# Two attention layers and two expert layers on one core: queries and keys held per sequence in a ring of four, values in nine columns a head, and expert outputs added to two sums in one tensor

## The chip, the cores and the metric

The kernel runs on one core of one Trainium2 chip. The metric is device time in microseconds (us). A core has TensorE (PE, with its weight loads shown as PEld), VectorE (DVE), ScalarE (ACT), GpSimd (POOL) and SyncE (SP), and 16 DMA engines. "SPq", "ACTq" and "POOLq" are DMAs issued from those engines.

## What is computed

Sixteen sequences of 256 tokens with 128 features pass through four layers with residuals, each on a layer norm of its input:

```python
x = x + attn_a(layernorm(x))   # 16 heads of 8, causal softmax(q k / sqrt(8)) v, projection
x = x + ffn(layernorm(x))      # 8 experts, the best two of each token, silu(x Wg) * (x Wu) @ Wd
x = x + attn_b(layernorm(x))   # 16 heads of 8, no mask
x = x + ffn(layernorm(x))      # the same expert weights
```

In attn_b the scores are an L2 form with one divisor per head and sequence:

```python
sim = -(q_row_2 - 2.0 * qk + k_col_2) / (fro_q * inf_xt)   # q_row_2 and k_col_2: maxima of a head
attn = softmax(sim)
```

The experts' outputs are weighted by the softmax of the two chosen router logits and scaled by 1/sqrt(12).

## The kernel before, in words

**Stages.** The kernel runs attention a, experts a, attention b, experts b and a last addition, one after another. Attention works on 8 blocks of 512 tokens (NT = 4 tiles of 128), that is two sequences a block. `project` (L535) loads a block (`loaded`, L522), normalizes it (`moments` L289, `normed` L303), transposes it, makes k and q with heads spread over partitions, splits each into a high and a low half in a short float format, and lays the halves by DMA (`lay`, L615) into the buffers `ks` and `qs`. There are three buffers of each, one a block, [128, 8, 512]. Eight DMAs of 256 KB lay a block: hi twice and lo twice, for k and for q. `vs` holds values with 32 columns a head, a one in the first, eight values and zeros after them.

**Rounds.** The stage is a list of 128 rounds, 16 a block and 8 a sequence; a round is one pair of heads of one sequence. In round `at` the program issues, in this order: `rows_scores` (L708), PE's scores of round `at` for the row maxima; `exponentials` (L771) of round `at - 14`, the transposed scores and ACT's exponential; `rows_maxima` (L725), one DVE reduction a round; in every second round `values` (L795) of round `at - 17`; and then the planner's steps. Row maxima are laid into spare rows of `qs` by `lay_maxima` (L740), so that the exponential's matmul subtracts them. Everything on PE, DVE, ACT, POOL and SP keeps its program order, so an instruction that waits holds up all behind it on its engine.

**The planner.** Side work is a set of generators: project, collect (L807), finish (L833), route (L332) and some set-up. Each yields how many rounds on it wants its next step, and of which kind. `due` (L866) runs at the end of each round. It takes the steps that are due, earliest first, and lets through one of kind BANK (which needs the spare PSUM banks), or two if more than two wait, and two that are not FREE (four if more than three wait). The rest come again in the next round. In attention b, project's steps stand 3, 1, 1, 2, 1, 1, 1, 1, 1, 1, 2 and 1 rounds after one another, from the load to the lay of q. Project of block n is due from round 16(n-1)-9 on in attention b, and 16(n-1)-8 in attention a (L916).

`collect` transposes the weighted values and divides by the row sums, `finish` applies the output projection and stores the block, and `route` normalizes it again, picks the two experts, and scatters each token's two rows into an HBM table by expert (POOL, eight indirect DMAs a block). In route the moments (DVE, then two small POOL operations for 1/sqrt) are followed one round later by the norm (DVE), at L337.

**Experts.** 39 tiles of 256 rows: load rows and weights, three matrix products, and POOL's indirect DMA with addition to the sums (`finish`, L1012). There are two sum tensors a layer, used in turn by the two halves of a tile; one starts as the residual, the other as zeros. `places` (L1001) makes the row numbers, with rows that no token owns sent to 128 spare rows.

**Set-up.** `prepared` (L274) sets k, q and v buffers to zero (POOL), lays ones, and is a planner task for the buffers 1 and 2, in rounds 0 to 12. `zeros` (L188) writes zeros to the sums. The last addition (from L1069) loads both sums block by block with 512-byte runs, adds and stores, all DMAs on SP's queue.

Of the kernel before, what the change touches and what calls it, by code (L numbers as in the profile page):

```python
# [42 lines left out]
P = 128  # L43
# [13 lines left out]
SEQ = 256  # L57
EPS = 1e-5
# [4 lines left out]
TOKENS = 4096  # L63
W = P + 2
# [6 lines left out]
def layers(  # L71
# [23 lines left out]
    ot = out.flatten_outer_dims().rearrange("(n t p) d -> n p t d", t=NT, p=P)  # L95
# [18 lines left out]
    def attention_weights(wq, bq, wk, bk, wv, bv, wo, bo, scale, name):  # L114
# [27 lines left out]
    blocks = ctx.enter_context(tc.tile_pool(name="blocks", bufs=4))  # L142
# [17 lines left out]
    half = const.tile([P, NE], F32, name="half")  # L160
# [14 lines left out]
    tokens = const.tile([P, NB * NT], F32, name="tokens")  # L175
    within = tokens[:, 0:ET]
    nobody = const.tile([P, 1], F32, name="nobody")
# [4 lines left out]
    totals = [  # L182
        [dram.tile([TOKENS + P, P], F32, name=f"total{i}{j}") for j in range(2)] for i in range(2)
    ]
    blank = const.tile([P, 3 * W], F32, name="blank")
    wr_sb = const.tile([P, NE], F32, name="wr_sb")

    def zeros():  # L188

        yield sy.dma_start(  # L190
            out=rows_in[NE * CAP : NE * CAP + TE, :].rearrange("(s p) d -> p s d", p=P),
            in_=blank[:, 0 : ET * W].rearrange("p (s d) -> p s d", s=ET),
        )
        for first, second in totals:
            flat = second.rearrange("(p a m) d -> p a (m d)", p=P, m=3)
            for k, m in ((0, 4), (4, 8), (8, 11)):
                to = flat[:, k:m, :]
                yield sy.dma_start(
                    out=to,
                    in_=blank[:, 0 : 3 * P].unsqueeze(1).to_broadcast([P, to.shape[1], 3 * P]),  # L200
                )
            yield sy.dma_start(out=first[TOKENS : TOKENS + P, :], in_=blank[:, 0:P])
# [3 lines left out]
    vs = [const.tile([P, NT, NH, HS], F32, name=f"v{i}") for i in range(3)]  # L206
    qs = [const.tile([P, NP, TB], F32R, name=f"q{i}") for i in range(3)]
    ks = [const.tile([P, NP, TB], F32R, name=f"k{i}") for i in range(3)]
# [30 lines left out]
    def later_constants():  # L239
# [19 lines left out]
        for t, pattern, base, by_partition in (  # L259
# [4 lines left out]
            (tokens, [[P, NB * NT]], 0, 1),  # L264
            (nobody, [[0, 1]], TOKENS, 1),
# [8 lines left out]
    def prepared(i):  # L274

        for t in (ks, qs) if i else ():
            for g in range(0, NP, 4):
                po.memset(t[i].bitcast(F32)[:, g : g + 4, :], 0.0)
                yield 1, FREE
        for j in range(2):  # L280
# [3 lines left out]
                in_=ones[0:2, :].unsqueeze(1).to_broadcast([2, NP * NT, P]),  # L284
            )
        po.memset(vs[i], 0.0)
        po.memset(vs[i].rearrange("p t h r -> p (t h) r")[:, :, 0:1], 1.0)
# [44 lines left out]
    def route(pool, psum, n, xb, free, sent):  # L332
# [4 lines left out]
        yield 1, BUSY  # L337
# [6 lines left out]
            tokens[:, n * NT : (n + 1) * NT].unsqueeze(1).to_broadcast([P, 2, NT]),  # L344
# [135 lines left out]
    def tokens_of(total, n):  # L480
        return total[n * TB : (n + 1) * TB, :].rearrange("(t p) d -> p t d", p=P)
# [27 lines left out]
    def attention(w, causal, name):  # L509
        with ExitStack() as own:  # L510
# [11 lines left out]
            def loaded(n):  # L522
# [5 lines left out]
                sy.dma_start(out=xb, in_=xt[n] if causal else tokens_of(totals[0][0], n))  # L528
                xs[n] = xb
                if not causal:  # L530
                    more = pool.tile([P, NT, P], F32, tag="more", bufs=1)
                    sy.dma_start(out=more, in_=tokens_of(totals[0][1], n))
                    return more

            def project(n):  # L535
# [38 lines left out]
                lay(ks[n % 3], halves(k, "k"), (0, 2, 1, 3))  # L574
                if causal:
                    yield 2, BANK
                    q = biased("wq", "bq", "q")
                    lay(qs[n % 3], halves(q, "q"), (0, 1, 2, 3), se if n == 0 else sy)
                else:
# [14 lines left out]
                    lay(qs[n % 3], (hi, lo), (0, 1, 2, 3), se if n == 0 else sy)  # L594
                    later(1, BUSY, constants(n, *rest))
                yield (2, BANK) if n else None
# [18 lines left out]
            def lay(to, parts, order, queue=sy):  # L615

                for i, slot in enumerate(order):
# [496 lines left out]
```

## Time and profile before

| | |
|---|---|
| median of 3 runs | 1337.88 us (1335.83 to 1341.29) |
| the profiled execution | 1343.86 us, span 1342.2 us |
| mean granted TensorE clock | 0.872 |
| busy in the span: PE, DVE, POOL, ACT | 79%, 59%, 44%, 39% |
| first scores of attention a, of attention b | 28.89, 690.46 us |
| first expert matmul, a and b | 423.69, 1088.44 us |
| issue of the last addition's first load | 1315.57 us |
| the row maxima's reduction, L222 (256 times) | 277.1 us busy |
| POOL's additions to the sums, L1019 (156 times) | 242.8 us busy |

Times in the profile are from the span's start. The attention code runs through one helper that keeps program order, so all of its instructions carry line L222 and are told apart by their tiles (mx, s, p, av, q, k). A row of the timeline gives the start, the busy time, the engine, the line, the operation, out<-in, the shape and a count; in brackets stands how long the engine was idle before, and what ended the wait. A row of busy time by stretch gives, for each engine, busy us and the number of instructions, then the granted clock, the DMA engines' share and GB/s. A busy PE is not PE at its peak.

### The profile page before, as it was taken

Reading aid. Unit: us, or ns where it says so; the run is one execution under the profiler, and the core shown is the slowest. Engines: PE = TensorE matmul, PEld = TensorE weight load, DVE = VectorE, ACT = ScalarE, POOL = GpSimd, SP = SyncE. Lnnn points to the kernel's source line nnn. Section 1 sums busy time; section 2 is a strip of 40 time slices with the busy share of each in tenths; the row PEclk is TensorE's granted clock in tenths of the full one; section 3 lists DMA queues with packets and bytes.
Section 4 is the critical chain, followed back from the end, with each engine's and each line's share of the span. In section 5 each row is a group of like instructions: output and inputs, shape, how many; then the busy total and the mean of one; then the engine's idle time right before and its main releaser. Section 6 shows DMA issues by size and latency. Waiting matters only on the chain. (4 is left out here: it accounts for less than half of the span.)

```text
span 1342.2 us, 23350 instructions
## 1 busy us (share of the span) xinstructions
PE 1066.8 (79%) x8116; PEld 771.8 (58%) x8116; DVE 787.6 (59%) x2221; ACT 518.8 (39%) x942; POOL 594.0 (44%) x599
## 2 busy tenths in 40 slices
PE   2799888898763999999457888778877459999990
PEld 1455555555543888888324454445554248888880
DVE  3667667776533555454258787888675535554541
ACT  1156445554521222222135756665555212222220
POOL 7444546655552555555330114233323325555551
PEclk9889878888855999999757999998788779999995
DMA  4244324530015877776253324133300087777757
GB/s 98 51 97 109 72 73 117 138 84 24 25 36 169 210 188 189 180 195 133 45 109 81 66 58 104 51 78 83 89 23 30 27 230 192 178 187 189 189 103 195
DMA packets 175301, 150.84 MB, mean 112 GB/s; under 512 B 14286, under 2 KB 136784, under 8 KB 175184
## 3 DMA queue, kind: packets, MB, share of 16 engines
q1 hardware_dynamic: 145310, 127.18, 34.8%
q0 software_dynamic: 26560, 18.76, 9.4%
q10 hardware_dynamic: 3314, 3.41, 1.1%
q8 instruction: 65, 1.06, 0.3%
q14 instruction: 52, 0.43, 0.1%
HBM read 82.74 MB, written 31.75 MB: 85 GB/s over the span
## 5 line engine op out<-in xcount | busy, mean ns | idle before, releaser
L1019 POOL DMA_INDIRECT total<-y,to x156 | 242.8, 1556 | 229.2 <-DVE here L1005 59.3
L222 DVE TENSOR_REDUCE mx<-s 128x6 f32<-128x768 f32 (+1 forms) x256 | 277.1, 1084 | 110.4 <-PE s L222 109.4
L222 ACT ACTIVATE p<-s 128x768 f32<-128x768 f32 (+1 forms) x256 | 232.9, 916 | 192.2 <-PE s L222 170.2
L1061 ACT ACTIVATE sg<-pg 128x256 f32<-128x256 f32 x312 | 119.4, 383 | 316.8 <-PE pg L1049 300.7
L1063 DVE TENSOR_TENSOR h<-pu,sg 128x256 f32<-128x256 f32 x312 | 131.9, 423 | 149.6 <-PE pu L1053 147.2
L222 POOL DMA_INDIRECT rows_in<-both_rows,slots x128 | 128.9, 1007 | 172.2 <-DVE both_rows L222 113.0
L1053 PE MATMUL pu<-xT,w_u 128*128 128x256 f32 x624 | 190.2, 387 | 5.7 <-DVE h L1063 5.5
L1049 PE MATMUL pg<-xT,w_g 128*128 128x256 f32 x624 | 192.6, 391 | 1.2 <-DMA w_g<-in_L_ffn_Wg_dram 0.7
L1028 PEld LDWEIGHTS py<-w_d,h 128*128 128x128 f32 x1248 | 163.8, 192 | 8.1
L1028 PE MATMUL py<-w_d,h 128*128 128x128 f32 x1248 | 164.6, 275 | 0.0
L222 PE MATMUL s<-k,q 62*128 62x256 f32 (+1 forms) x1024 | 144.3, 367 | 16.1 <-DMA k<-lo 11.4
L222 PE MATMUL s<-q,k 64*128 64x256 f32 (+1 forms) x1024 | 114.2, 307 | 42.1 <-DVE mx L222 33.5
L222 PE MATMUL av<-p,v 128*32 128x256 f32 (+1 forms) x2048 | 144.5, 406 | 0.3 <-ACT au L222 0.2
L222 PEld LDWEIGHTS s<-k,q 62*128 62x128 f32 x1024 | 89.2, 216 | 87.7 <-issue 51.8
L1053 PEld LDWEIGHTS pu<-xT,w_u 128*128 128x128 f32 x624 | 118.0, 192 | 29.6 <-DVE h L1063 13.8
L222 POOL TENSOR_SCALAR_AFFINE_SELECT p<-p 128x512 f32<-128x512 f32 x128 | 82.5, 645 | 108.3 <-ACT p L222 103.7
L222 PEld LDWEIGHTS s<-q,k 64*128 64x128 f32 x1024 | 89.5, 213 | 58.9 <-DVE mx L222 39.7
L1049 PEld LDWEIGHTS pg<-xT,w_g 128*128 128x128 f32 x624 | 102.2, 194 | 20.3 <-issue 13.8
L222 PEld LDWEIGHTS av<-p,v 128*32 128x32 f32 x2048 | 58.7, 120 | 55.2 <-issue 26.4
L222 POOL TENSOR_TENSOR lo<-to,hi 128x512 fp32r<-128x512 f32 x24 | 30.6, 1273 | 72.4 <-ACT hi L222 72.3
L996 PE MATMUL ps<-ident,x_in 128*128 128x128 f32 x156 | 30.6, 279 | 39.1 <-DMA x_in<-rows_in 39.1
L222 PE MATMUL s<-mask_q,ident_h 128*128 128x256 bf16 x256 | 58.6, 317 | 0.0
(206 smaller groups left out, 1179.3 us busy)
## 6 DMA issues: line engine op xcount, KB each, us to landing
w_g<-in_L_ffn_Wg_dram SPq DMA_DIRECT2D x78, 256.0 KB
w_u<-in_L_ffn_Wu_dram SPq DMA_DIRECT2D x78, 256.0 KB
w_d<-in_L_ffn_Wd_dram SPq DMA_DIRECT2D x78, 256.0 KB
x_in<-rows_in SPq DMA_DIRECT2D x78, 130.0 KB
k<-hi SPq DMA_DIRECT2D x32, 256.0 KB
k<-lo SPq DMA_DIRECT2D x32, 256.0 KB
q<-hi SPq DMA_DIRECT2D x28, 256.0 KB
q<-lo SPq DMA_DIRECT2D x28, 256.0 KB
```

The lines of the kernel that those rows point to most:

```text
L222: return tc.keep_in_program_order(method(*args, **kwargs))
L996: nc.tensor.transpose(ps[:, bass.ts(s, P)], x_in[:, s, 0:P], ident)
L1019: nc.gpsimd.indirect_dma_start(out=sums[(i * ET + s) % 2], out_offset=bass.IndirectOffsetOnAxis(ap=to[:, s : s + 1], axis=0), in_=y[:, s, ...
L1028: nc.tensor.matmul(py[:, s, :], lhsT=hs[c][:, bass.ts(s, P)], rhs=w_d[:, c, :], start=c == 0, stop=c == NC - 1,)
L1049: nc.tensor.matmul(pg, lhsT=w_g[:, bass.ts(c, P)], rhs=this, start=True, stop=True)
L1053: nc.tensor.matmul(pu, lhsT=w_u[:, bass.ts(c, P)], rhs=this, start=True, stop=True)
L1061: nc.scalar.activation(sg, pg, AF.Silu)
L1063: nc.vector.tensor_tensor(h, pu, sg, ALU.mult)
```

## The change

1. `ks` and `qs` become rings of four buffers, one a sequence ([128, 8, 256]). A block is laid in two parts: the first sequence where it was laid before, the second as a planner task of its own, eight rounds later (`lay_second`). Project starts at 16(n-1)-5 in attention b and 16(n-1)-3 in attention a, since a slot must be free; block 1 of attention a stays at -8. Buffers 0 and 1 are set to zero at the start, 2 and 3 in the first rounds.
2. `vs` has nine columns a head in place of 32, and one PSUM tile `av` serves a whole stage, set to zero once.
3. Route's norm comes three rounds after its moments, in place of one.
4. Each layer has one tensor with two sums, one below the other. A token's first choice adds to the first and its second choice to the second, so that each row takes one addition, and the additions are declared free of order among themselves. Rows without a token go to 8 x 128 spare rows. The first loads of the next reader wait for all additions by hand.
5. The last addition reads and stores four adjacent rows a partition (2 KB runs) and uses SP's and ACT's queues. There is a fifth block buffer and a fourth for its partner.

```diff
+RING = 4
+IDLE = 8
-    blocks = ctx.enter_context(tc.tile_pool(name="blocks", bufs=4))
+    blocks = ctx.enter_context(tc.tile_pool(name="blocks", bufs=5))
-    totals = [
-        [dram.tile([TOKENS + P, P], F32, name=f"total{i}{j}") for j in range(2)] for i in range(2)
-    ]
+    totals = [dram.tile([2 * TOKENS + IDLE * P, P], F32, name=f"total{i}") for i in range(2)]
-    vs = [const.tile([P, NT, NH, HS], F32, name=f"v{i}") for i in range(3)]
-    qs = [const.tile([P, NP, TB], F32R, name=f"q{i}") for i in range(3)]
-    ks = [const.tile([P, NP, TB], F32R, name=f"k{i}") for i in range(3)]
+    vs = [const.tile([P, NT, NH, 1 + HD], F32, name=f"v{i}") for i in range(3)]
+    qs = [const.tile([P, NP, SEQ], F32R, name=f"q{i}") for i in range(RING)]
+    ks = [const.tile([P, NP, SEQ], F32R, name=f"k{i}") for i in range(RING)]
...
     def prepared(i):
-        for t in (ks, qs) if i else ():
-            for g in range(0, NP, 4):
-                po.memset(t[i].bitcast(F32)[:, g : g + 4, :], 0.0)
+        for t in (ks[i], qs[i]):
+            if i > 1:
+                po.memset(t.bitcast(F32), 0.0)
                 yield 1, FREE
...
-        po.memset(vs[i], 0.0)
-        po.memset(vs[i].rearrange("p t h r -> p (t h) r")[:, :, 0:1], 1.0)
...
         mv, rstd = yield from moments(pool, xb)
-        yield 1, BUSY
+        yield 3, BUSY
...
+    def wait_for(load, scatters):
+        for scatter in scatters:
+            tc.add_manual_dep(
...
                 if not causal:
-                    more = pool.tile([P, NT, P], F32, tag="more", bufs=1)
-                    sy.dma_start(out=more, in_=tokens_of(totals[0][1], n))
+                    more = pool.tile([P, NT, P], F32, tag="more" if n else "o", bufs=1)
+                    second = (sy if n else se).dma_start(out=more, in_=tokens_of(totals[0], 1, n))
+                    for on in (load, second) if n == 0 else ():
+                        wait_for(on, landed)
...
-                lay(ks[n % 3], halves(k, "k"), (0, 2, 1, 3))
+                k_parts = halves(k, "k")
+                lay(n, 0, ks, k_parts, (0, 2, 1, 3))
...
-                    lay(qs[n % 3], (hi, lo), (0, 1, 2, 3), se if n == 0 else sy)
+                    q_parts = hi, lo
+                    lay(n, 0, qs, q_parts, (0, 1, 2, 3), se if n == 0 else sy)
                     later(1, BUSY, constants(n, *rest))
+                then = lay_second(n, k_parts, q_parts)
+                if n == 0:
+                    for _ in then:
+                        pass
+                else:
+                    later(8 if n > 1 else 1, FREE, then)
...
+            def lay(n, b, to, parts, order, queue=sy):
+                assert at >= (2 * n + b - RING + 1) * each // 2 + lag or 2 * n + b < RING
+                to = to[(2 * n + b) % RING].bitcast(F32)
                 for i, slot in enumerate(order):
                     queue.dma_start(
+                        out=to[slot : slot + P - SLOTS + 1 : SLOTS, :, :],
+                        in_=parts[i // 2].bitcast(F32)[:, b * SEQ : (b + 1) * SEQ],
                     )
+            def lay_second(n, k_parts, q_parts):
+                lay(n, 1, ks, k_parts, (0, 2, 1, 3))
+                yield 1, FREE
+                lay(n, 1, qs, q_parts, (0, 1, 2, 3))
...
-                            av[i * HS : (i + 1) * HS, f % 2, lo:SEQ],
+                            av[i * HS : i * HS + 1 + HD, f % 2, lo:SEQ],
...
-                for n in range(1, 3):
-                    later(8 * n - 8, FREE, prepared(n), 0)
+                for i in range(2, RING):
+                    later(0, FREE, prepared(i), 0)
...
-                later(max(0, (n - 1) * each - (8 if causal else 9)), FREE, project(n))
+                later(max(0, (n - 1) * each - (8 if n == 1 else 3 if causal else 5)), FREE, project(n))
...
-                nc.vector.tensor_scalar(here, within, left[:, i : i + 1], None, ALU.is_lt)
+                none = nobody[:, i * ET % IDLE : i * ET % IDLE + ET]
                 nc.vector.scalar_tensor_tensor(
-                    here, x_in[:, :, P], nobody, here, ALU.subtract, ALU.mult
+                    here, within, left[:, i : i + 1], none, ALU.is_ge, ALU.mult
                 )
-                nc.vector.tensor_scalar(to, here, nobody, None, ALU.add)
+                nc.vector.tensor_tensor(to, here, x_in[:, :, P], ALU.add)
...
-                    nc.gpsimd.indirect_dma_start(
-                        out=sums[(i * ET + s) % 2],
+                    add = nc.gpsimd.indirect_dma_start(
+                        out=total,
...
+                    tc.declare_no_dep(add.ins, group=group, reason="a row takes one addition")
...
+                def rows_of(of, n):
+                    return of.rearrange("(p n m) d -> n p m d", p=P, m=NT)[n]
                 for n in range(NB):
                     a = blocks.tile([P, NT, P], F32, tag="xb")
-                    nc.sync.dma_start(out=a, in_=tokens_of(sums[0], n))
-                    b = pool.tile([P, NT, P], F32, tag="b", bufs=3)
-                    nc.sync.dma_start(out=b, in_=tokens_of(sums[1], n))
+                    b = pool.tile([P, NT, P], F32, tag="b", bufs=4)
+                    for i, t, queue in ((0, a, nc.sync), (1, b, nc.scalar)):
+                        load = queue.dma_start(out=t, in_=rows_of(total[i * TOKENS : (i + 1) * TOKENS, :], n))
+                        if n == 0:
+                            wait_for(load, added)
                     nc.vector.tensor_tensor(a, a, b, ALU.add)
-                    nc.sync.dma_start(out=ot[n], in_=a)
+                    (nc.sync, nc.scalar)[n % 2].dma_start(out=rows_of(out.flatten_outer_dims(), n), in_=a)
```

## The prediction, made before the result was known

> **What bounds the kernel now.** I read the page first: slices of PE, PEclk and DMA. The span has four parts: attention a (0 to about 400 us), experts a (423 to 647), attention b (690 to 1045 with its lead-in from 652), experts b (1086 to 1310), then a tail. Busy time by stretch came second.
>
> ```profile
> core 0: us, PE busy (x) PEld busy (x) DVE busy (x) ACT busy (x) POOL busy (x), PEclk, DMA share, GB/s
> 690.00:1045.00 355.00, 283.30 (x2537) 172.38 (x2536) 271.86 (x714) 210.41 (x336) 98.16 (x109) 0.87 0.28 67
> 1317.60:1342.20 24.60, 0.00 (x0) 0.00 (x0) 5.54 (x8) 0.00 (x0) 0.00 (x0) 0.50 0.87 247
> ```
>
> Attention b has no full engine: PE 80%, DVE 77%, ACT 59%. Its engines wait for one another, in order, so a late operand delays the whole chain. The tail has no compute; its 24.6 us are DMA at 0.87 of the 16 engines. In the experts' stretch 1100 to 1200 the same view has PE at 98.68 of 100 us: TensorE sets the pace, 5.5 us a tile, and POOL's additions lie beside it.
>
> Third, the timeline of one round of attention b (PE, DVE and SP), where block 3's q is laid:
>
> ```profile
> 782.05 0.50 PE L222 MATMUL s<-k,q 62*128 62x256 f32 x4
> 784.37 0.50 PE L222 MATMUL s<-k,q 62*128 62x256 f32 x4
> ...
> 781.97 1.22 DVE L222 TENSOR_REDUCE mx<-s 128x4 f32<-128x1024 f32 x1
> 783.59 0.87 DVE L222 SCALAR_TENSOR_TENSOR lo<-to,by,hi 128x256 fp32r<-128x256 f32 x2
> 784.38 1.22 DVE L222 TENSOR_REDUCE mx<-s 128x4 f32<-128x1024 f32 x1
> ...
> 783.78 1.18 SPq L222 DMA_DIRECT2D q<-hi  x2
> 785.05 1.24 SPq L222 DMA_DIRECT2D q<-lo  x2
> ```
>
> PE makes the scores of the next round while DVE reduces this one. The reduction at 781.97 is the 42nd of the stage (round 41): block 3 starts in round 48, so its q is laid 7 rounds ahead. Fourth, attention a, where PE did wait for a lay, and where it waited behind a memset:
>
> ```profile
> 40.62 3.55 POOL L222 MEMSET k<- 128x2048 f32 x2
> 40.83 5.73 DVE L222 TENSOR_SCALAR xn<-xb,mv,rstd 128x128 f32<-128x128 f32 x4
> 46.13 1.09 PE L222 MATMUL ps<-ident,xn 128*128 128x128 f32 x4 [5.33 <-DVE xn L222]
> ...
> 63.80 1.24 SPq L222 DMA_DIRECT2D q<-hi  x2
> 65.14 1.18 SPq L222 DMA_DIRECT2D q<-lo  x2
> 71.16 0.72 PE L222 MATMUL s<-k,q 62*128 62x128 f32 x4 [1.88 <-DMA q<-lo]
> ```
>
> So a lay of 1 MB releases PE 7.4 us after its first issue and 4.8 us after its last (66.32 to 71.16), and a wait for it is real.
>
> **Part 1: the ring of four.** A block has 16 rounds. I walked the planner's list by its rules, round by round, before and after. Before, the walk gives q's lay 7 rounds ahead for blocks 2 to 7 of attention b, as the trace has it. After, project starts 21 rounds ahead of its block, not 25. Its steps need 16 rounds if nothing holds them, so q could be laid 5 ahead. But they now fall on the rounds in which collect, finish and route want the one BANK step a round (and route itself ends two rounds later), and the delay grows from 2 rounds to 5. Offsets of the lay from the block's first round:
>
> - block 2: q -3; second sequence k +5, q +6
> - block 3: q -1; k +7, q +8
> - blocks 4 to 7: q 0; k +8, q +9
>
> The second sequence's scores start in round +8. A step runs after its round's scores. So in rounds 0 (blocks 4 to 7), 8 and 9 the scores read the slot's old contents. That moves only the maxima, which shift the softmax, and costs nothing. The next round reads the new data, and PE waits for the DMA with exponentials and values queued behind it. That wait is the main new cost:
>
> - First q. From the reduction's start (781.97) lo is done 2.49 us on and the four issues are over 4.32 us on (786.29). Landing after the last issue is unseen for half the bytes: at most 4.8 (the whole 1 MB above), at least 2.5 (the page's median for a small row scatter); I take 3.0, towards the smaller since the bytes halve. Scores 0.5: next reduction at 7.8 instead of 2.4 (784.38). Loss 5.4 us in blocks 3 to 7; block 2 has three rounds and loses none.
> - Second k, blocks 4 to 7: issued when the round's scores are done (T), four issues of 0.6, landing 3, scores 0.5: T+5.9. Normal: T+1.8+2.8 (a round) = T+4.6. Loss 1.3.
> - Second q stands on SP's queue behind the next block's k (its hi after ACT, its lo after POOL): projection to T+2.1, an exponential 1.0, to 0.69 and hi 0.62 give about T+4.6, POOL's lo 1.27 behind a row scatter 1.3 gives T+7.2, q's four issues T+9.6, landing and scores T+13.1. Normal after the k's loss is T+8.7: loss 4.4 in blocks 4 to 6. Block 3's k is in time, so its normal is T+4.6 and it loses 8.5. Block 7 has no next k: it loses 3.1.
>
> Sum: 13.9 + 3 x 11.1 + 9.8 = 57 us. Low end 25: SP starts sooner than I think, or idle time of DVE (23%) gives half back. High end 90: landing 4.8, and half clock after each wait (the same score group takes 0.79 us at the stage's slow moments, 0.50 at its fast ones). In attention a the walk puts q 5 to 8 ahead and the second pair at +1 to +4; at 2.8 us a round that covers the 7 to 14 us from step to landing: 0, at worst 3 each for six blocks.
>
> The Trainium skill ("TensorE: Matmul & The Clock Gate", Part 1) says that an idle window of about 3.4 us brings TensorE to half rate until a busy one follows. The transitions here show a granted 0.59 to 0.64, and the tail 0.50. By that rule ten waits would cost an estimated 10 us more; I leave it in the high end.
>
> **Part 2: the first rounds.** Memsets of k and q shrink from eight of 1.81 us after the start to four, all within rounds 0 and 1; the three of v (1.81 each) become strided ones (0.2). The transform that took 5.73 us beside a POOL memset takes about 1.1 elsewhere (753.72): 4.5 us. A wait of 1.6 behind the q memset at 55.81 goes: together -6 (0 to -7). The first scores wait 11.4 us for k<-lo until 28.89; half the bytes must land: -3 (0 to -5). Block 1's 1.88 us above: -1.5 (0 to -1.9).
>
> **Part 3: route.** DVE waits 20.4 us for rstd over 11 times, 3.3 of it in 690 to 1045 and 10.0 in 120 to 390 (waits of these stretches). Two more rounds remove nearly all of it, but in attention a PE is the fuller engine: -4 (0 to -10).
>
> **Part 4: values.** Nine columns load as weights beside the matmuls, which move the same 256 columns: 0 both ways within 3 us (weight loads of av are 58.7 us in all, under PE).
>
> **Part 5: additions.** One DVE operation a tile less and no order between additions. DVE's 11.8 us of waits for an addition are 0.27 each, PE is 98.7% busy: -2 (0 to -5). The first loads of attention b now both wait for the last addition, where xb's started 3.2 us earlier (652.19 against 655.38): +1 (0 to +2).
>
> **Part 6: tail.** 6.29 MB in 512-byte runs: the trace's DMA records have 27 to 28.5 ns a packet, 12,288 of them on 16 engines, 21.9 us. Runs of 2 KB take 84 to 99 ns in the expert stages: 16.1 to 18.9 us. That saves 3.0 to 5.8, less the head start of the first load (1315.57): -3.5 (0 to -6). The Trainium skill ("DMA: Bandwidth & Descriptors", Why small descriptors are slow) puts the cost of short runs at about 3 cycles a packet beside one per 32 bytes: by it four packets of 512 bytes take 76 cycles where one of 2 KB takes 67, an estimated 2.6 us saved, less than the rows give.
>
> **Sum.** -6 -3 -1.5 -4 -2 +1 -3.5 = -19; +57: +38. Against the profiled execution (span 1342.2, time 1343.9) that is 1382; the median shown, 1337.88, lies 6 lower, so 1376.
>
> **The rivals.**
> - Late lays are hidden (0.24). If project's BANK steps get through earlier than in my walk, or the waits are absorbed by the 20 to 23% that PE and DVE idle, only the savings stay: 1337.9 - 19 = 1319, up to 1330. It decides when q of blocks 4 to 7 is issued three or more rounds ahead. For it: DVE's own waits in b are short. Against: the 1.88 us wait above came with a lay four rounds ahead.
> - Waits and gains cancel (0.08): the stalls end at 20, time 1332 to 1344. The low end of Part 1 with all gains.
> - SP's queue decides (0.10): k's lo stands behind several row scatters on POOL, as at 810.12 to 815.91, where k<-lo is issued 5.8 us after k<-hi, and every second q slips by that: 90 us, gains 10, time 1418.
> - My forecast (0.58): 1345 to 1410.
>
> Within 0.5% of 1337.9 is about what a measurement of this kernel can't tell from no change. Faster by more: the first rival, 0.24. Same: 0.08. Slower: 0.68. The range leaves out a tenth at each end: 1318 to 1418; without the faster cases it would be 1345 to 1418.
>
> **What would show it.** Right: attention b grows by some 50 us, with PE score groups idle behind DMA q<-lo and DMA k<-lo, three times a block from block 4 on, and lower PEclk there; attention a ends some 10 us sooner; no transform of 5 us near 41; a tail near 21. Wrong: attention b as long as now, and DMA behind no score. The sum also fails if attention a gains waits of its own.

## The result, and the profile after

The changed kernel takes **1411.09 us** (median of four runs, 1407.02 to 1415.71) against 1339.59 for the kernel before beside it (1335.83 to 1345.46): a ratio of **1.053** (95% interval 1.048 to 1.058), slower. The forecast was 1376, in a range of 1318 to 1418: the sign and the range hold, the forecast is 35 us low, and the time lies just above the 1345 to 1410 that were given for it. The profiled execution has a span of 1411.1 us (time 1412.84) against 1342.2. So 68.9 us are to be explained.

The busy time by stretch comes first again. The rows are the 128 rounds of attention b and the tail.

```profile
core 0: us, PE busy (x) PEld busy (x) DVE busy (x) ACT busy (x) POOL busy (x), PEclk, DMA share, GB/s
669.80:1086.80 417.00, 289.74 (x2337) 170.01 (x2335) 263.60 (x663) 194.40 (x314) 87.62 (x98) 0.76 0.20 55
1389.30:1411.10 21.80, 0.00 (x0) 0.00 (x0) 5.54 (x8) 0.00 (x0) 0.00 (x0) 0.50 0.81 289
```

The same 128 rounds of the kernel before:

```profile
691.30:1020.30 329.00, 262.50 (x2333) 160.14 (x2335) 260.20 (x662) 193.68 (x315) 88.77 (x98) 0.87 0.29 70
```

DVE, ACT and POOL do the same work within 4 us, in 88 us more, so the engines wait. PE's busy time is 27 us longer, at a granted clock of 0.76 in place of 0.87. What PE waits for is in the list of waits of the changed kernel (engine and tile, what ended the wait; total us, times, longest), in attention b:

```profile
DVE mx L221 <- PE s L221: 105.0, 41, 10.6
PE s L221 <- DMA q<-lo: 55.6, 11, 9.4
PE s L221 <- DMA k<-lo: 19.1, 5, 4.4
PEld s L221 <- DMA q<-lo: 12.2, 2, 6.1
```

So PE's scores wait 74.7 us for lays, 16 times (the weight loads, PEld, wait in some of the same moments). The kernel before has no DMA of q or k in its list there, and DVE waits 31.6 us for scores. Where the 68.9 us lie, from the starts of the first and last reductions, the first expert matmuls and the first load of the last addition that waits for all additions of experts b (1317.58 before, 1389.30 after):

| us | before | after | difference | on record |
|---|---|---|---|---|
| start to a's first reduction | 30.3 | 26.7 | -3.6 | -3 |
| a's rounds | 324.1 | 302.5 | -21.6 | -7.5, and a part of route's -4 |
| a's last reduction to the first expert matmul | 69.4 | 74.0 | +4.6 | 0 |
| experts a and b's lead-in | 267.6 | 266.6 | -1.0 | -1 |
| b's rounds | 329.0 | 417.0 | +88.0 | +57 |
| b's last reduction to the first expert matmul | 68.1 | 70.8 | +2.7 | 0 |
| experts b | 229.1 | 231.7 | +2.6 | 0 |
| tail | 24.6 | 21.8 | -2.8 | -3.5 |

The loss has the place that was named, and one and a half times the size. Block 4 shows it in the changed kernel. From the timelines of SP, DVE and PE, around the second sequence's start:

```profile
891.36 1.18 SPq L221 DMA_DIRECT2D k<-hi  x2
892.59 1.25 SPq L221 DMA_DIRECT2D k<-lo  x2
895.17 1.18 SPq L221 DMA_DIRECT2D k<-hi  x2
897.26 1.17 SPq L221 DMA_DIRECT2D k<-lo  x2
898.53 1.21 SPq L221 DMA_DIRECT2D q<-hi  x2
899.79 1.46 SPq L221 DMA_DIRECT2D q<-lo  x2
...
891.37 1.23 DVE L221 TENSOR_REDUCE mx<-s 128x4 f32<-128x1024 f32 x1 [0.53 <-PE s L221]
896.46 1.23 DVE L221 TENSOR_REDUCE mx<-s 128x4 f32<-128x1024 f32 x1 [3.06 <-PE s L221]
904.70 1.23 DVE L221 TENSOR_REDUCE mx<-s 128x4 f32<-128x1024 f32 x1 [7.01 <-PE s L221]
...
895.92 0.50 PE L221 MATMUL s<-k,q 62*128 62x256 f32 x4 [3.13 <-DMA k<-lo]
903.87 0.79 PE L221 MATMUL s<-k,q 62*128 62x256 f32 x4 [4.67 <-DMA q<-lo]
```

SP issues the second k, then the next block's k (895.17), and only then the second q: the order that the walk gave. The rounds that begin at 891.37 and 896.46 take 5.1 and 8.2 us. The rounds of blocks 4 to 6, in mean us from one reduction to the next and summed by position in the block, are the measure for much that follows:

| round | 0 | 1 to 3 | 4 to 7 | 8 | 9 | 10 to 15 | block |
|---|---|---|---|---|---|---|---|
| before | 1.3 | 10.0 | 12.5 | 3.8 | 2.5 | 15.8 | 45.8 |
| after | 6.8 | 14.1 | 12.4 | 5.1 | 7.9 | 15.1 | 61.4 |

### The profile page after: what moved, and what is told of

Its sections match the earlier page's. It is cut to its first block, busy times and chain, and to the rows that moved or that the text cites. A ratio compares the mean times of both kernels' runs of the same rounds, so it can differ in the third digit from the quotient of the medians.

```text
span 1411.1 us, 23498 instructions
## 1 busy us (share of the span) xinstructions
PE 1083.3 (77%) x8116; PEld 771.8 (55%) x8116; DVE 773.3 (55%) x2146; ACT 517.5 (37%) x942; POOL 579.5 (41%) x593
## 4 chain that ended last, share of the span: by engine, by line
PE 19%; DVE 11%; POOL 8%; issue 7%; DMA 6%; SPq 2%; ACT 2%; POOLq 0%; DVEq 0%; ACTq 0%
PE ps L221 6%; POOL total L1044 6%; PE s L221 5%; DVE mx L221 4%; PE av L221 3%; DMA q<-lo 2%; SPq L221 2%; PE pu L1082 2%; PE pg L1078 2%; PE py L1057 2%; DMA total<-y,to 1%; POOL rows_in L221 1%; DVE term L221 1%; DMA k<-lo 1%; DMA b<-total 1%
## 5 line engine op out<-in xcount | busy, mean ns | idle before, releaser
L221 PE MATMUL s<-k,q 62*128 62x256 f32 (+1 forms) x1024 | 148.6, 377 | 93.7 <-DMA q<-lo 58.0
L221 PEld LDWEIGHTS s<-k,q 62*128 62x128 f32 x1024 | 93.0, 225 | 167.6 <-issue 106.4
L221 PE MATMUL av<-p,v 128*9 128x256 f32 (+1 forms) x2048 | 155.3, 423 | 4.6 <-POOL p L221 2.9
L221 PE MATMUL s<-q,k 64*128 64x256 f32 (+1 forms) x1024 | 119.4, 317 | 39.8 <-DVE mx L221 33.6
L1082 PEld LDWEIGHTS pu<-xT,w_u 128*128 128x128 f32 x624 | 118.0, 193 | 31.6 <-DVE h L1092 15.8
L221 PEld LDWEIGHTS s<-q,k 64*128 64x128 f32 x1024 | 93.4, 221 | 59.0 <-DVE mx L221 43.0
L1078 PEld LDWEIGHTS pg<-xT,w_g 128*128 128x128 f32 x624 | 102.0, 193 | 20.9 <-issue 14.1
L221 PEld LDWEIGHTS av<-p,v 128*9 128x9 f32 x2048 | 48.6, 98 | 73.3 <-issue 37.6
```

What stands on the lines that cost most here:

```text
L221: return tc.keep_in_program_order(method(*args, **kwargs))
L1078: nc.tensor.matmul(pg, lhsT=w_g[:, bass.ts(c, P)], rhs=this, start=True, stop=True)
L1082: nc.tensor.matmul(pu, lhsT=w_u[:, bass.ts(c, P)], rhs=this, start=True, stop=True)
```

## The experiments

**Theory A**: the lateness of the lays costs the time, as on record. **Theory B**: splitting the lays costs it (twice as many DMAs, of half the size, on the same queue). Times stand beside the kernel before on the same chip, whose median was between 1339.6 and 1355.0; so ratios are compared, and stages of the profiled executions.

### Early: the ring, without the lateness

```diff
-RING = 4
+RING = 6
-        yield 3, BUSY
+        yield 1, BUSY
-                later(max(0, (n - 1) * each - (8 if n == 1 else 3 if causal else 5)), FREE, project(n))
+                later(max(0, (n - 1) * each - (8 if n == 1 else 3 if causal else 9)), FREE, project(n))
```

> The changed kernel with six buffers for sequences instead of four, project of blocks 2 to 7 of attention b started nine rounds ahead as in the kernel before, and route's norm one round after its moments. By the planner's rules the first q is then laid 7 rounds ahead of its use and the second k and q 7 and 6 rounds ahead; the lays stay split in two, the values stay at nine columns, the additions and the tail stay as changed. Theory A (the lateness of the lays costs the time): the rounds of attention b shrink from about 418 us to the 329 of the kernel before, within 12, the waits of PE's scores for q<-lo and k<-lo in b fall from 92 us to under 15, the clock there rises from 0.76 to 0.83 or more; total 1411 - 89 + 4 (route) = 1326, between 1315 and 1340. Theory B (twice as many lays of half the size, or their place on SP's queue, cost it): the time stays above 1385.

1326.82 us, ratio **0.985** (0.977 to 0.994): faster than before. Attention b's rounds take 337.9 us. In the list of waits, all that PE's scores still wait there for q or k is

```profile
PE s L221 <- DMA q<-lo: 0.8, 1, 0.8
```

The waits for lays are gone, the clock of the stretch is back at 0.85, with the lays still in two parts. Theory B falls.

### Late only: the lateness, without the ring

```diff
-                later(max(0, (n - 1) * each - (8 if causal else 9)), FREE, project(n))
+                later(max(0, (n - 1) * each - (8 if causal else 5)), FREE, project(n))
```

in the kernel before.

> The kernel before with one number changed: project of blocks 2 to 7 of attention b starts five rounds ahead in place of nine. Its q is then laid in round 0 of blocks 3 to 7, all eight DMAs of a block as before. Theory A: one late lay a block. On record 5.4 us a block for half the bytes, 7.2 with the whole ones, five blocks: +36, and if each wait brings the clock down with it, up to +55; total 1365 to 1400, with PE's scores waiting for q<-lo about five times. Theory B: no part of the split or of the ring is in it, so no change: 1336 to 1348.

1403.95 us, ratio 1.040 (1.033 to 1.048). One number makes attention b 392.5 us long, 63.5 more. PE waits five times, once a block, as the walk says, and each wait is like this one (scores, then values):

```profile
857.45 0.80 PE L222 MATMUL s<-k,q 62*128 62x256 f32 x4 [9.49 <-DMA q<-lo]
...
858.60 1.93 PE L222 MATMUL av<-p,v 128*32 128x256 f32 x16
```

In blocks 4 to 6 round 0 takes 8.1 us in place of 1.3: 6.8 lost where 7.2 was expected. But a block takes 55.8 in place of 45.8. So the waits themselves are some 34 of the 63.5 us; the rest comes after them and in the blocks ahead (blocks 0 and 1 27.7 and 45.0 us against 29.5 and 36.0, block 2 48.2 against 42.5), where project's steps now fall on other rounds.

### Second at once: only the first sequence late

```diff
-RING = 4
+RING = 6
-                    later(8 if n > 1 else 1, FREE, then)
+                    later(8 if n > 1 and causal else 1, FREE, then)
```

> The changed kernel with six buffers, and in attention b the second sequence laid one round after the first in place of eight; project still starts five rounds ahead. So q of the first sequence is as late as in the changed kernel (round 0 of blocks 4 to 7) and the second k and q are 7 and 6 rounds early. Theory A with the sizes on record (second k 1.3 and second q 4.4 to 8.5 a block, 30 us in all): 1411 - 30 = 1381. Theory A with equal prices for each of the three waits of a block: two thirds of 89 come back, 1352 (1340 to 1365). Theory B: 1400 or more.

1386.36 us, ratio 1.028 (1.019 to 1.036); span 1382.6, the size on record (1381) to 2 us. Attention b is 25.7 us shorter than in the changed kernel. PE's waits for k are gone; those for the first q stay (29.3 us in five). So the three waits of a block are not equally dear: the second pair costs 26 us in all (30 on record), and what stays, 62 us, goes with the late first q and with project's late start, where the record had 27.

### Route with one round

```diff
-        yield 3, BUSY
+        yield 1, BUSY
```

in the changed kernel.

> The changed kernel with route's norm one round after its moments, in both attention stages, as before the change. On record: the two rounds more are worth 4 us (0 to 10), so this takes 1415 (1411 to 1421); DVE waits for rstd again some 20 us in all. By the planner's rules the lays of attention b move by at most one round (block 3's q from -1 to 0, its second pair from 7 and 8 to 8 and 9). Rival: the longer route keeps more steps of kind BANK in the list and is itself part of the loss in b: then 1405 or less. If attention a's unpredicted gain (21.5 us, 11.5 predicted) came from route, attention a gets 5 to 10 us longer.

1405.96 us, ratio 1.042 (1.033 to 1.051): not 4 us longer; 5 us shorter than the changed kernel's 1411, with intervals that touch. In attention a DVE waits 4.9 us for rstd with one round here, and 5.2 with three in the changed kernel (12.8 in the kernel before, with one): what went was not route's doing. Attention b's rounds take 409.0 us in place of 417.0. In its blocks 4 to 6 the three waits stay about as they were (rounds 0, 8 and 9 take 6.5, 5.3 and 8.1 us), but rounds 1 to 3 take 10.4 in place of 14.1, and a block 57.9 in place of 61.4. So in these two profiles, one of each, route's added rounds are a part of b's loss, as the expectation's rival had it. The lead-out of a, from its last reduction to the first expert matmul, is 67.8 to 69.9 us in all nine profiles with one round, and 71.3 to 74.6 in all five with three: the last block's route ends later, some 4 us.

### Rank: four buffers, project first

```diff
-                later(max(0, (n - 1) * each - (8 if n == 1 else 3 if causal else 5)), FREE, project(n))
+                later(max(0, (n - 1) * each - (8 if n == 1 else 3 if causal else 4)), FREE, project(n), 1 if causal else 0)
-                    later(8 if n > 1 else 1, FREE, then)
+                    later((8 if causal else 3) if n > 1 else 1, FREE, then)
```

> The changed kernel with its four buffers, but in attention b project's steps go first in the planner's list (as those of the row maxima do), project starts four rounds ahead in place of five, and the second sequence is laid three rounds after the first in place of eight. By the planner's rules the first q is laid in round -4 of its block, the second pair in rounds -1 and 0, eight or more ahead of their use; route's steps wait a few rounds longer. Theory A (lateness alone, brought about by project standing behind route, collect and finish): b's rounds come back to 330 to 345 us, total 1325 to 1345, with no need of more buffers. Rival (four buffers of one sequence are too few, since a lay then waits for the exponentials that read the slot): scores or lays wait for the slot and b stays above 370, total above 1365.

1338.92 us, ratio 0.997 (0.993 to 1.002). Project starts even later than in the changed kernel, but its steps don't stand behind route, collect and finish, and the second lay comes ahead of the next block's k. Attention b takes 343.3 us at a clock of 0.84, and no q or k is in PE's list of waits any more. Its longest item is the scores' wait for a free buffer, that is for DVE:

```profile
PE s L221 <- DVE mx L221: 45.0, 34, 5.7
```

So four buffers are enough, and project's late start alone is not the loss: what counts is how late the lays come out of the list. The run changes project's rank and the second lay's eight rounds together, and does not say what each is worth.

### Fill, and fill more: what the clock costs

In late only, matmuls were put on PE ahead of the scores that wait:

```diff
+                if not causal and n > 2 and b == 0 and g == 1:
+                    for _ in range(30):
+                        te.matmul(
+                            s[:, 0, 0:SEQ], lhsT=ident_h, rhs=mask_q.rearrange("p c m -> p (c m)"),
+                            start=True, stop=True,
+                        )
```

> The kernel before with project five rounds ahead in attention b (as in the run late_only), and 30 more matmuls of 128x256 in a short float format, about 0.22 us each, put on PE in round 1 of blocks 3 to 7, ahead of the scores that wait for q; their result is overwritten. They fill some 6.6 of the 9.5 us of each wait and change nothing else. Theory of the clock (part of the loss is half rate after each wait): the scores after the wait take 0.50 in place of 0.80 us, PE's busy time in b without the added matmuls goes back towards 264 from 283 us, and the time falls by 8 to 16 us against late_only's 1404, to 1388 to 1396, although work is added. Theory of the wait alone: the added work lies in the wait, so the time is that of late_only, within 4 us, or longer.

1399.00 us, ratio 1.039 (1.027 to 1.051). The added matmuls took half the time that I had taken (3.45 us for 30), so 6.1 us of idle stayed and the scores after it still took 0.79. It tells nothing apart. With 78:

> As the run fill, with 78 added matmuls in place of 30: there they took 0.115 us each, 3.45 us of the wait, 6.1 us of idle were left, and the scores after it still took 0.79. 78 take 9.0 of the 9.5 us, so PE is never idle for long ahead of the scores. Theory of the clock: the scores after the wait now take 0.50, values 1.07 in place of 1.93, rounds 1 to 3 of blocks 4 to 6 lose some 2 us (11.8 us in late_only), and the whole 392 us of attention b becomes 375 to 385. Theory of the wait alone: rounds 1 to 3 stay at 11 to 12 us and b at 388 to 396; what follows a wait is then DVE's work that was held up (route, constants, statistics), and not the clock.

1404.06 us, ratio 1.043 (1.035 to 1.051). Now the same group as above reads

```profile
862.37 8.69 PE L222 MATMUL s<-mask_q,ident_h 128*128 128x256 bf16 x78
...
872.29 0.50 PE L222 MATMUL s<-k,q 62*128 62x256 f32 x4 [1.24 <-DMA q<-lo]
...
872.96 1.07 PE L222 MATMUL av<-p,v 128*32 128x256 f32 x16
```

Scores and values run at the full rate (0.50 and 1.07 for 0.80 and 1.93), and the granted clock of b is 0.86 for 0.77. But b takes 385.8 us: 6.7 less than late only, and 0.9 less than fill, where the clock after a wait was low. Rounds 1 to 3 take 11.7 us, as they did (11.8). So in these profiles the clock after the waits is worth no more than 7 us in five waits, and the ratios of late only, fill and fill more (1.040, 1.039, 1.043) do not differ beyond their intervals; the theory of the wait alone is the nearer one.

### Load early: the stall of the first rounds

```diff
-                yield 3, FREE
+                yield (3 if causal or n < 2 else 7), FREE
-                later(max(0, (n - 1) * each - (8 if n == 1 else 3 if causal else 5)), FREE, project(n))
+                later(max(0, (n - 1) * each - (8 if n == 1 else 3 if causal else 9)), FREE, project(n))
```

in the changed kernel. These are the lines of SP and POOL there that it is about:

```profile
693.59 0.59 SPq L221 DMA_DIRECT2D xb<-total  x1
703.50 0.37 SPq L221 DMA_DIRECT2D more<-total  x1
...
706.22 1.26 POOL L221 TENSOR_TENSOR xb<-xb,more 128x512 f32<-128x512 f32 x1 [25.49 <-DMA more<-total]
```

In the trace the DMAs of SP and ACT share eight semaphores, and the issue of one waits for the semaphore that it is going to use, that is until the previous DMA on it has landed. That of `more` at 703.50 is ACT's lay of row maxima, issued at 701.24; SP's list of waits has q<-turned with 9.3 us there.

> The changed kernel, in which the loads of a block's two sums in attention b are issued nine rounds ahead as before the change, and all other steps of project where the change put them. In the changed kernel block 2's load of the second sum is held up for 9.3 us by an earlier DMA of ACT's queue, POOL's addition waits 25.5 us for it, DVE 10.9 us behind that, and the first eight rounds of b take 38.6 us against 29.5 before. Theory: that load, issued late and behind twelve lays, is the whole of the surplus in blocks 0 and 1 (about 10 us), so the first eight rounds take 28 to 31 us and the total falls by 6 to 11, to 1400 to 1405; the late lays of blocks 2 to 7 stay as they are. Rival: the surplus comes from the burst of lays itself; no change, or the stall moves to another DMA: 1408 to 1415.

1407.86 us, ratio 1.049 (1.039 to 1.058). (The expectation's "first eight rounds" are block 0, sixteen rounds; the figures are block 0's.) Block 0 takes 27.4 us in place of 38.6, as expected. But block 1 takes 40.6 in place of 36.2 and block 3 62.9 in place of 57.4: b's rounds take 414.4 us, 2.6 less. The stall's cause is shown; what its removal gave was mostly given back.

### Two more: three rounds ahead

```diff
-RING = 4
+RING = 5
-                later(max(0, (n - 1) * each - (8 if n == 1 else 3 if causal else 5)), FREE, project(n))
+                later(max(0, (n - 1) * each - (8 if n == 1 else 3 if causal else 7)), FREE, project(n))
```

> The changed kernel with five buffers and project seven rounds ahead in attention b. By the planner's rules the first q is laid in round -3 (three ahead of what block 0 of the next needs), the second k and q in rounds +5 and +6, three and two ahead of their use at round 8. On record: three or more rounds ahead hides the lays. So of 89 us only the second q's rest (two rounds ahead, 5.6 us of cover against some 8: 2 to 3 us a block, 10 to 15 in all) and the stall of the first rounds (10) stay: total 1411 - 65 = 1346 (1335 to 1360). If a lay needs more than three rounds, PE's scores still wait for q<-lo ten times and the time is above 1370.

1379.10 us, ratio 1.031 (1.021 to 1.041): above 1370, the expectation fell. The first q is hidden but for some 1 us a block, but five second q's are not. SP and PE near the second sequence's start of block 3:

```profile
807.49 1.17 SPq L221 DMA_DIRECT2D k<-hi  x2
808.83 1.19 SPq L221 DMA_DIRECT2D k<-lo  x2
810.07 1.24 SPq L221 DMA_DIRECT2D q<-hi  x2
811.36 1.25 SPq L221 DMA_DIRECT2D q<-lo  x2
...
815.43 0.80 PE L221 MATMUL s<-k,q 62*128 62x256 f32 x4 [7.75 <-DMA q<-lo]
```

The k at 807.49 is the next block's, whose hi comes out of PE and ACT in that round. The second q, ready for nine rounds, stands behind it on SP's queue, and PE then waits 7.3 to 7.8 us in each of blocks 3 to 6. Rounds ahead are no cover if a waiting DMA stands in front on the queue.

### Nine columns, no ring, and early again

Nine has part 4 alone in the kernel before:

```diff
-    vs = [const.tile([P, NT, NH, HS], F32, name=f"v{i}") for i in range(3)]
+    vs = [const.tile([P, NT, NH, 1 + HD], F32, name=f"v{i}") for i in range(3)]
-                            av[i * HS : (i + 1) * HS, f % 2, lo:SEQ],
+                            av[i * HS : i * HS + 1 + HD, f % 2, lo:SEQ],
```

with one av tile a stage and the column of ones set alone.

> The kernel before with part 4 of the change alone: values in nine columns a head, one av tile a stage set to zero once, and of v only the column of ones set at the start. On record: 0 within 3 us for the values, and up to 2 us for the memsets of v: 1334 to 1343 by the kernel before's 1338 (or the same distance from its time on this chip). Rival: the smaller weight loads let PE run at a higher granted clock in attention a, where the kernel before showed 0.85 in one profile and its copies (the runs late_only and fill, with the same attention a) 0.93 and 0.86, and all seven profiles with nine columns 0.90 to 0.93: then its clock from 100 us on is 0.90 or more and attention a's 128 rounds take 300 to 310 us in place of 317 (mean of three).

1349.97 us, ratio 1.002 (0.997 to 1.006): nothing, as on record. Attention a's rounds take 315.8 us. The rival falls.

No ring is the changed kernel with whole blocks:

```diff
-    qs = [const.tile([P, NP, SEQ], F32R, name=f"q{i}") for i in range(RING)]
+    qs = [const.tile([P, NP, TB], F32R, name=f"q{i}") for i in range(3)]
-                in_=parts[i // 2].bitcast(F32)[:, b * SEQ : (b + 1) * SEQ],
+                in_=parts[i // 2].bitcast(F32),
-        yield 3, BUSY
+        yield 1, BUSY
```

and the same for k, the memsets, the lays and project's start as before.

> The changed kernel without part 1 and part 3: three buffers of a whole block for queries and keys, eight DMAs of 256 KB a block, project eight and nine rounds ahead, the buffers set to zero as before, and route's norm one round after its moments. What stays is the nine columns, the unordered additions, the wait of the first loads and the tail. On record these are 0 (values), -2 (additions), +1 (first loads), -3.5 (tail) and a part of -6 (v's memsets): -5 to -9 against the kernel before. Theory A (the ring itself costs nothing, only the lateness it brought): within 10 us of the run early, which has a ring of six and the same rest. Rival (laying by sequence, in smaller DMAs, is a gain in itself): the run early is faster than this one by more than 10 us, since there the halves are awaited later and the memsets are shorter.

1354.03 us, ratio 1.002 (0.998 to 1.006).

> The run early once more, beside the others of this call: a ring of six, project nine rounds ahead in attention b, route's norm one round after its moments, all else as changed. There it took 0.985 of the kernel before (0.977 to 0.994). Theory A: again faster than the kernel before by 1 to 2%, 1318 to 1330, and so faster than both kernels.

1325.54 us, ratio **0.982** (0.977 to 0.988), and 28 us less than no ring. Early is the version that beats both kernels. The two differ in attention a; first the 128 rounds of no ring, then of early:

```profile
30.50:350.30 319.80, 273.65 (x2541) 167.01 (x2545) 218.11 (x534) 149.72 (x224) 166.95 (x216) 0.86 0.35 85
```

```profile
26.60:325.80 299.20, 257.77 (x2541) 160.18 (x2545) 211.23 (x535) 149.12 (x224) 170.34 (x218) 0.91 0.35 93
```

Up to its last reduction, attention a is 24.5 us shorter (3.9 ahead of the first reduction, 20.6 in the rounds), and b the same within 2 us. In a they differ in the ring alone and in what goes with it (smaller lays and memsets, project three rounds ahead and not eight). So the rival of that run holds: queries and keys by sequence, with what goes with them, are the gain that this change holds, and the other parts together give nothing that these runs can tell.

## Why the prediction was right, and where it was wrong

**Part 1, right in mechanism, wrong in size: +57 on record, +88 measured.** The walk's offsets for blocks 3 to 7 and the order on SP's queue came out as written, and so did the waits, but for two more: block 2's second q (1.7 us) and block 3's second k (4.2 us), which was said to be in time. Term by term, from the table of rounds (blocks 4 to 6):

- First q 5.4: round 0 measures +5.5. That the two agree is partly luck: on record the round went from 2.4 to 7.8 us with 3.0 from the last issue's end to the scores, and it went from 1.3 to 6.8, with 1.9 to 2.0 (859.78 to 861.66 in block 4), so that two errors of some 1 us cancel. Second k 1.3: round 8 measures +1.3. Second q 4.4: round 9 measures +5.4. Block 7, 9.8 on record, is 9.5 longer (46.9 against 37.4).
- The mis-sized term is the sum over a block: 11.1 on record, 15.6 measured. The surplus stands in rounds 1 to 3, which had nothing on record and take 14.1 us in place of 10.0. DVE is busy for 10.2 us there in place of 6.1, since steps of layer norm, constants and route's best choice now fall on these rounds, and it waits for scores as well. I took each wait to end with its own round, but that a wait by itself costs this much afterwards isn't shown: route one has the same three waits, and with 10.4 us in these rounds its block takes 12.0 more than before, near the sum on record. So by these two profiles most of the surplus goes with route's two added rounds, whose steps I moved in the walk and gave no price in b.
- Blocks 0 to 2 were on record at 0. Blocks 0 and 1 lose 9.3 (nearly all in block 0, where the load waits for a semaphore), and block 2 loses 11.3 (of which block 3's first q, laid in round -1, waits 5.7 us at the end of block 2). So 13 us of blocks 4 to 6, 9 of blocks 0 and 1 and 11 of block 2 are the surplus, less 3 in block 3. In the total, some 10 us of it are hidden by attention a, whose rounds gained 21.6 us where 11.5 were on record.

**The clock.** It fell to 0.76 as feared, PE was busy 27 us longer, and that looked like the answer. Fill more, with the clock brought back, shows no more than 7 us for five waits. The rule of the Trainium skill ("TensorE: Matmul & The Clock Gate", Part 1) that an idle window brings half rate agrees with the traces (0.80 for 0.50 after 9.5 us of idle, 0.50 after 1.24). By it the prediction had an estimated 10 us for ten waits, in the high end; the 7 for five, which is a bound, doesn't contradict it. Here the slower matmuls lay mostly beside other work.

**Part 2 and attention a.** The first scores gave -3.6 (-3 on record). Blocks 0 and 1 took 66.8 us in place of 74.2: -7.4, against -6 and -1.5. Blocks 2 to 7 gave 14 us more that were on record only as a share of route's 4. All eight profiles with lays by sequence have 296 to 304 us for a's rounds, all six with whole blocks 307 to 324, with nine columns or without, with route at one round or three. The difference is clear in the first scores and in blocks 0 and 1 (62 to 67 us against 73 to 74), some 11 us together. In blocks 2 to 7 the two groups overlap, and the time goes with the granted clock. These are blocks 2 to 7 in the kernel before, in late only, whose attention a is the same code, and in early again:

```profile
104.50:354.30 249.80, 219.80 (x2079) 138.04 (x2083) 171.35 (x444) 123.83 (x184) 135.63 (x179) 0.85 0.33 84
104.50:337.60 233.10, 202.87 (x2079) 129.54 (x2083) 171.32 (x444) 123.51 (x184) 135.75 (x179) 0.93 0.35 90
91.60:325.80 234.20, 201.65 (x2083) 126.33 (x2087) 171.12 (x457) 122.92 (x185) 136.51 (x181) 0.93 0.35 95
```

In late only, whole blocks are as fast there as the ring, at the same clock. All eight profiles with the ring have 0.91 to 0.93 in these blocks, those with whole blocks 0.85 to 0.89 but for late only. Whether the ring brings the higher clock, and how, stays open.

**Part 3**, -4 on record, is the step with the wrong sign: rstd's wait in a is the same with one round or three, the lead-out of attention a gets about 4 us longer, and b is 8 us longer with three than in route one.

**Parts 4 to 6.** Values 0 (nine: 1.002). Additions -2: experts a, from their first matmul to the load that waits for the last addition, took 229.7 us for 231.7, but experts b took 231.7 for 229.1, so no gain shows over both. First loads +1: b's lead-in took 36.9 for 35.9. Tail -3.5: 21.8 for 24.6, so -2.8. Before, one load had been issued 2.0 us ahead of that count (1315.57); from the first load on, the tail takes 21.8 us for 26.6, which is -4.8, inside the 3.0 to 5.8 of the rows. The 2.6 estimated from the Trainium skill ("DMA: Bandwidth & Descriptors", Why small descriptors are slow) is less than that, but the change also uses a second queue and more buffers, and no run here has the longer runs alone.

**The rivals.** That late lays are hidden was said to decide at three rounds ahead. Two more shows this point wrong: ahead in the list is not ahead on the queue. SP's queue was the third rival, with POOL's scatters as its place; the queue is indeed part of it, but the instruction in front is the next block's k. By luck its 90 us in b are nearer to the 88 than my 57: what it assumed, k<-lo issued 5.8 us after k<-hi, did not come (2.1 us in block 4, 895.17 and 897.26).

## What to carry to other kernels

A smaller buffer can bring two things: shorter transfers and set-up, with a gain that was 28 us here and is understood only in part, and a later start, which can cost more; measure them apart by keeping the old start with enough buffers. Where a planner shares slots among tasks, a step that others wait for may need a rank of its own, not only an earlier due time, and a transfer that is ready should not be issued behind one that isn't. A sum over waits is not the whole price of a later start: the side work moves to other rounds too, and a delay added elsewhere in the same list (here route's) can cost in a stage where it was given no price.

## What was not expected of the hardware

- Lays in packets of half the size move at the same rate. In the DMA records, 186 to 205 packets of 1,024 bytes start in each microsecond from 690 to 695 us of the changed kernel, and 96 or 97 of 2,048 bytes from 695 to 697 us of the kernel before: about 200 GB/s both, so the runs of 1 KB cost nothing here. But half a lay is not released in half the time: PE's scores of a block start 1.9 to 2.1 us after the end of the last issue of the first q in the changed kernel, and 3.1 to 3.8 us after it in late only, with twice the bytes.
- A load on SP's queue was held for 9.3 us by a small DMA of ACT's queue, through a semaphore that the two share in the program. With more and smaller DMAs, the same eight semaphores come round sooner.
- A lower granted clock (0.77 for 0.86, late only and fill more) went with an attention b that was 2% longer (392.5 and 385.8 us): PE's rate was hardly the bound there.
- The same code of attention a took 233 us in blocks 2 to 7 in one profile and 249 to 250 in three others, at a granted clock of 0.93 and of 0.85 to 0.86. So a difference of this size in one pair of profiles need not come from the edit.
